# A graph layer's first attention step: the threshold guess formed as a logarithm, three guards in front of the mask, and list places found with one comparison

## The chip, the cores and the metric

The kernel runs on one NeuronCore of a Trainium2 chip. The time is that of the device in microseconds (us), from the start of the execution to its end; each time below is the median of several runs, or belongs to one profiled execution where that is said. The engines are TensorE (PE; PEld is its weight load), VectorE (DVE), ScalarE (ACT), GpSimd (POOL) and SyncE (SP, which here only issues DMAs).

## The reference

3327 nodes have 256 features each. The layer normalises the rows, cuts them at zero, and sends them through two steps of a graph layer; each step does this:

```
q = Xa @ W1.T @ W2.T;  k = Xa @ W3.T            # 64 wide
probs = softmax(q @ k.T)                         # 3327 x 3327
keep the largest entries of each row until their sum reaches 0.9; renormalise
Xf = R @ Xf        # R: the sparse adjacency plus identity, rows normalised
Xa = A @ Xa        # A: the kept probabilities
Z += Xf @ U1[n].T + Xa @ U2[n].T
```

At the end comes a layer norm of X + Z and a residual. So each row needs a threshold: the value from which on its entries are kept. The adjacency has only a few nonzero entries in each row; the kernel finds them as lists and fetches the few blocks it needs.

## The kernel before, in words

The nodes are cut into 26 tiles of 128 rows (the last one has fewer). Two steps follow each other: step 0 (about 60 to 745 us of the profiled execution) and step 1 (from there to the end). Only step 0 is touched here.

In step 0 each tile t goes through these stages, and the loop of `guess_graph_layer` over i keeps several tiles in flight at once:

- **weights** (L583 to L610): PE forms the logits `pl`, ACT takes their exponential into `e` (128 x 3328) and sums each row.
- **measured_once** (L635 to L666): ACT guesses from the row's sum Z and a fitted law where the threshold may lie (`guessed`, L616 to L625, and L640 to L642, one number per row in the columns of a small tile `g`); GpSimd prepares four more numbers (L643 to L646); ACT then makes two whole passes over `e` (L633: Relu and Sign, each with a row sum), which tell the mass below the guess. Seven small ACT operations (L653 to L659) turn this into a better guess, and five small VectorE operations (L662 to L666) add guards and write it to column 16.
- **settle** (L723 to L767): VectorE takes the part of `e` below the guess into `w` (L729), finds its largest entries by MAX8 over 20 segments (L734) and five rounds over the candidates (L741, L743), derives from them the exact threshold (L748 to L753), and cuts the row with it, the **mask** (L763, in place in `e`).
- **Sums** (L809 to L832): PE transposes the masked `e` four blocks at a time into `pt` (L809), ACT copies them to `eT` (L811), PE multiplies them with the nodes into `pa` (L823).
- **first_end** and **prep** (L474 to L502, L937 to L949): products with U2, new keys and queries (`pz`, `pk`, `pg`).

Beside this the adjacency is turned into lists. `listed` (L836 to L868) reduces the blocks of `adj` that SP loads, and leaves up to 16 neighbour numbers per row in `lists`; the first four are fetched directly, further ones by an overflow column that all rows share. VectorE counts a row's overflow entries into `over` (L865). `packed` (L870 to L880) turns the counts into places: PE adds the counts of the rows before (`pb`, with the matrix `upto`), and VectorE writes a 0/1 matrix `oh` with two comparisons, so that oh[row, n] is 1 where the row's first place <= n < first place + count. `gathered` (L882 to L894) multiplies with `oh` on PE (`po`), ACT copies the result (`lo` L888, `nth` L890), VectorE picks (L893), GpSimd writes the index (L894). GpSimd then issues indirect DMAs: five per tile for adjacency blocks (`ac`, L900) and five for node rows (`xg`, L921). `diffuse` multiplies the two (`pr`, L929), and `spread` finishes on VectorE (L1118, L1119).

The order of the work on each engine is the order of the text: at the end of `guess_graph_layer` every instruction of PE, ACT, VectorE and GpSimd is tied to the one before it. Each letter of the strings in PLAN and BEGIN stands for one stage and runs it up to its next `yield`; a tile of step 0 has seven such strings. The letters that count here are m (measured_once), d (settle), p (packed), h (gathered), g (one indirect DMA, which also waits for the ACT instruction that precedes it in the text), w and q (weights). A stage that has pieces left at the end of a turn is run out there. So the last piece of m, VectorE's guards, ran at the end of a turn, behind the mask of the tile before.

The pool `ps_t` has two PSUM buffers, which `pt`, `po`, `pq`, `pk`, `pg`, `pb` use in turn; so PE's `pk` (L485) waits until ACT has copied `mq` out of `pq` (L532), and a `pt` behind `po` waits for `nth`.

If any row's threshold can't be proved, a flag makes the program run a second, slow layer (`search_graph_layer`) at the end.

Of the kernel before, what the change touches and what calls it, by code (L numbers as in the profile page):

```python
# [9 lines left out]
F32 = mybir.dt.float32  # L10
# [3 lines left out]
AF = mybir.ActivationFunctionType  # L14
ALU = mybir.AluOpType
# [3 lines left out]
P = 128  # L19
# [4 lines left out]
NP = NT * P  # L24
# [288 lines left out]
BIG = 1.0e30  # L313
# [6 lines left out]
OFFSET = (18.0, 14.0)  # L320
TOPK = 8 * max(ROUNDS)
LNY = 0.25 * math.log(0.72)

SQG, SQK = ((c[0], c[1] / (2 * c[0]), c[2] - c[1] ** 2 / (4 * c[0])) for c in (PG, PK))
# [12 lines left out]
DIRECT = 4  # L337
LIST = 16
# [7 lines left out]
def guess_graph_layer(ctx, tc, x, adj, w1t, w2t, w3t, u1t, u2t, ln_g, ln_b, out, flag):  # L346
# [18 lines left out]
    valid = lambda t: 0 <= t < NT  # L365
# [47 lines left out]
    one = const.tile([P, 8], F32, tag="one", name="one")  # L413
    for k, c in enumerate((1.0, -1.0, 5.0e-4, SQG[1], SQK[1], math.log(10.0), LNY, 1.0e-12)):
        G.memset(one[:, k : k + 1], c)
# [212 lines left out]
    def con(k):  # L628
        return one[:, k : k + 1]
# [5 lines left out]
    def measured_once(r):  # L635
# [200 lines left out]
    def listed():  # L836
# [10 lines left out]
        for k, (t, j0, n) in enumerate(pieces):  # L847
# [6 lines left out]
            if j0 + n < NT:  # L854
# [9 lines left out]
            of = small.tile([P, LIST], F32, tag="of", name="of", bufs=2)  # L864
# [3 lines left out]
            yield  # L868

    def packed(t):  # L870

        assert t in done
# [3 lines left out]
        S.copy(ls[:, LIST:], pb[:, 0, :1])  # L876
        yield
        ohs[t] = oh = small.tile([P, P], F32, tag="oh", name="oh", bufs=2)
        V.tensor_scalar(oh, place, ov, ls[:, LIST:], ALU.subtract, ALU.is_lt)
        V.scalar_tensor_tensor(oh, place, ls[:, LIST:], oh, ALU.is_ge, ALU.mult)  # L880

    def gathered(t):  # L882
# [10 lines left out]
        V.scalar_tensor_tensor(of[:, :n], place[:, :n], nth, lo, ALU.is_equal, ALU.mult, accum_out=nth)  # L893
        G.tensor_scalar(index[:, t, DIRECT:], nth, -1.0, float(NONE), ALU.mult, ALU.add)  # L894
# [88 lines left out]
    live, ohs, acs, xgs, done, early = {}, {}, {}, {}, [], {}  # L983
# [45 lines left out]
    for q in range(HALF + 5):  # L1029
# [40 lines left out]
        if 0 <= q - 4 < HALF and 2 * (q - 4) in COUNTED:  # L1070
            k = q - 4
# [54 lines left out]
    def refetch(t):  # L1126
# [9 lines left out]
    PLAN = (("gmdsssa", "gmcdsssa", "edawwpg", "gmsdga", "gmspdea", "ohgdawwqg", "gehmgq"),  # L1136
# [5 lines left out]
             0: ("mdbb", "mcdbb", "medbwwbp", "mdbb", "gmpdbwwb", "hgdbgbq", "hgq"),  # L1142
             1: ("ggmdsssbb", "gmcdgsssbb", "gedbwwbp", "bmsdg", "gmpdeg", "hgdwwqg", "hgemgqo"),
             2: ("gmdsssa", "gmcdsssga", "gedawwpg", "gmsdga", "gmspdea", "ohgdawwqg", "gehmgq")}
# [136 lines left out]
```

## Time and profile before

| | us |
|---|---|
| median of 3 runs | 1347.66 (1346.17 to 1348.82) |
| the profiled execution, its own time | 1349.25 |
| its span, first to last instruction | 1347.5 |
| busy in the span: PE, PEld | 1269.8 (94%), 975.5 (72%) |
| busy in the span: DVE, ACT, POOL | 1187.0 (88%), 1080.0 (80%), 1002.8 (74%) |
| chain that ended last, by engine | PE 50%, DVE 27%, ACT 14%, POOL 3%, issue 3%, DMA 2% |

The granted TensorE clock was 0.982 of full speed as a mean. A row of the profile names line, engine and operation, then output<-input, how often, the busy time in us, the mean duration in ns, and the idle time of the engine ahead of it with what ended it. The chain of waits follows the last instruction back to what it waited for. Everything that concerns step 0 is read from the windows between 0 and 745 us.

### The profile page before, as it was taken

To read this page: it belongs to the slowest core of one execution; us is meant where nothing else is said; L and a number is where in the kernel's file an instruction comes from. 1 tells how busy PE (TensorE), PEld (TensorE's weight loads), DVE (VectorE), ACT (ScalarE), POOL (GpSimd) and SP (SyncE) were. 2 spreads that over 40 slices of the span, in tenths; PEclk is the share of its full clock that TensorE was granted. 3 is DMA by queue.
4 is the path that set the end of the run, shared out by engine and by line. 5 is a ranking of instruction groups with operands and counts; after the bars stand their busy time and mean duration, and the time that the engine had idled before them with its cause. 6 is when DMAs were issued, how large, how long until landed. Compare 5 with 4: busy or idle time off the path is not lost.

```text
span 1347.5 us, 22277 instructions
## 1 busy us (share of the span) xinstructions
PE 1269.8 (94%) x6495; PEld 975.5 (72%) x6495; DVE 1187.0 (88%) x3637; ACT 1080.0 (80%) x2368; POOL 1002.8 (74%) x1399
## 2 busy tenths in 40 slices
PE   5989999999999999999999579999998999999985
PEld 4635777778777787777877457777777777777774
DVE  6867899999999999999991699899998999999993
ACT  5476798888878888888853889899998999999931
POOL 5214888888888888887873588888888888888822
PEclk9999999999999999999999789999999999999988
DMA  8734455454554545545432212121222212122100
GB/s 278 226 124 140 133 146 158 133 159 128 140 158 132 156 135 144 151 135 149 122 105 82 81 48 83 55 90 55 92 77 65 87 56 91 59 86 89 54 20 24
DMA packets 92645, 149.79 MB, mean 111 GB/s; under 512 B 15425, under 2 KB 59072, under 8 KB 92512
## 3 DMA queue, kind: packets, MB, share of 16 engines
q1 hardware_dynamic: 75056, 105.37, 24.7%
q0 software_dynamic: 16640, 42.69, 12.4%
q8 instruction: 54, 0.88, 0.3%
q14 instruction: 79, 0.65, 0.2%
q10 hardware_dynamic: 816, 0.20, 0.1%
HBM read 120.93 MB, written 27.28 MB: 110 GB/s over the span
## 4 chain that ended last, share of the span: by engine, by line
PE 50%; DVE 27%; ACT 14%; POOL 3%; issue 3%; DMA 2%; SPq 0%; POOLq 0%; DVEq 0%; ACTq 0%
PE pa L823 22%; ACT ja L633 7%; PE pl L600 7%; PE pt L809 6%; DVE w L729 5%; PE pr L929 5%; DVE cand L734 4%; DVE e L763 4%; PE pz L942 3%; DVE bb L741 2%; DVE cand L743 2%; DVE x L763 2%; PE pz L1011 2%; ACT eT L811 1%; ACT e L604 1%
## 5 line engine op out<-in xcount | busy, mean ns | idle before, releaser
L823 PE MATMUL pa<-xw,eT 128*128 128x256 f32 x1352 | 323.1, 383 | 3.3 <-DVE s L953 3.3
L633 ACT ACTIVATE ja<-e,g 128x3328 uint8<-128x3328 f32 x106 | 325.8, 3073 | 0.1
L823 PE MATMUL pa<-x,eT 128*128 128x256 f32 x1352 | 322.0, 379 | 0.0
L823 PEld LDWEIGHTS pa<-xw,eT 128*128 128x128 f32 x1352 | 250.5, 190 | 52.0 <-issue 14.4
L823 PEld LDWEIGHTS pa<-x,eT 128*128 128x128 f32 x1352 | 242.8, 190 | 25.5
L734 DVE MAX8 cand<-w 128x8 f32<-128x168 f32 (+1 forms) x1040 | 253.3, 317 | 0.0
L921 POOL DMA_INDIRECT xg<-bx,index x130 | 200.9, 1546 | 52.8 <-issue 24.4
L811 ACT COPY eT<-pt 128x512 f32<-128x512 f32 (+1 forms) x364 | 199.8, 556 | 46.6 <-PE pt L809 45.9
L809 PE MATMUL pt<-ident,e 128*128 128x128 f32 x1144 | 177.0, 277 | 16.8 <-DVE e L760 9.3
L900 POOL DMA_INDIRECT ac<-in_adj,index x130 | 147.8, 1137 | 58.4 <-issue 26.6
L809 PEld LDWEIGHTS pt<-ident,e 128*128 128x128 f32 x1144 | 140.3, 145 | 60.3 <-issue 33.1
L729 DVE SCALAR_TENSOR_TENSOR w<-e,g 128x3328 f32<-128x3328 f32 x44 | 163.4, 3715 | 2.8 <-ACT g L714 2.7
L921 POOL DMA_INDIRECT xg<-vx,index x130 | 133.3, 1025 | 34.1 <-issue 30.0
L763 DVE SCALAR_TENSOR_TENSOR e<-e,rec 128x3328 f32<-128x3328 f32 x40 | 151.3, 3782 | 0.6
L929 PE MATMUL pr<-xg,ac 128*128 128x257 f32 (+1 forms) x520 | 142.4, 398 | 8.2 <-DVE s L1119 6.5
L604 ACT ACTIVATE e<-pl 128x832 f32<-128x832 f32 x132 | 112.9, 859 | 22.4 <-PE pl L600 19.0
L929 PEld LDWEIGHTS pr<-xg,ac 128*128 128x128 f32 x520 | 94.7, 196 | 34.3 <-issue 14.4
L600 PE MATMUL pl<-both,qT 64*128 64x416 f32 x416 | 93.0, 546 | 8.0 <-ACT e L604 4.3
L741 DVE MAX8 bb<-cand 128x8 f32<-128x160 f32 x286 | 92.6, 324 | 6.4
L600 PE MATMUL pl<-after,qT 64*128 64x416 f32 x416 | 95.7, 554 | 0.5 <-ACT e L604 0.5
L853 DVE TENSOR_REDUCE fm<-at 128x4 f32<-128x512 f32 (+1 forms) x133 | 84.3, 634 | 0.3 <-DMA at<-in_adj 0.3
L946 POOL TENSOR_TENSOR sv<-sv,x 128x256 f32<-128x256 f32 x26 | 65.5, 2518 | 13.4 <-ACT sv L945 12.1
(260 smaller groups left out, 2163.4 us busy)
## 6 DMA issues: line engine op xcount, KB each, us to landing
at<-in_adj SPq DMA_DIRECT2D x114, 256.0 KB
cx<-ac SPq DMA_DIRECT2D x26, 384.0 KB
ac<-cx SPq DMA_DIRECT2D x26, 384.0 KB
wide<-in_adj SPq DMA_DIRECT2D x8, 832.0 KB
e<-in_adj SPq DMA_DIRECT2D x6, 832.0 KB
own<-bx SPq DMA_DIRECT2D x26, 128.5 KB
x<-in_x SPq DMA_DIRECT2D x13, 256.0 KB
xr<-in_x SPq DMA_DIRECT2D x26, 128.0 KB
```

The lines of the kernel that those rows point to most:

```text
L600: PE.matmul(pl[:, a, :wd], qT[p, :], keys_of(step, a).rearrange("p a b -> p (a b)")[:, c : c + wd], start=True, stop=True)
L604: S.activation(e.rearrange("p (a n) -> p a n", a=2)[:, :, c : c + wd], pl[:, :, :wd], AF.Exp, accum_out=za[:, n : n + 1])
L633: S.activation(ja, e, f, bias=guess, scale=sign, accum_out=total)
L729: V.scalar_tensor_tensor(w, e, col(16), e, ALU.is_lt, ALU.mult, accum_out=d2)
L734: V.max(cand[:, 8 * s : 8 * s + 8], w[:, s * SEG : min(NP, (s + 1) * SEG)])
L763: V.scalar_tensor_tensor(e, e, at(1), e, ALU.is_ge, ALU.mult, accum_out=ra)
L809: PE.transpose(pt[:, j, :], e[:, (j0 + j) * P : (j0 + j + 1) * P], ident)
L811: S.copy(eT[:, :w, :], pt[:, :w, :])
L823: PE.matmul(self.pa, eT[:, c - 4 * k, :], self.xa[:, j, :], start=c == 0, stop=c == NT - 1)
L900: G.indirect_dma_start(out=ac[:, k, :], out_offset=None, in_=rows, in_offset=bass.IndirectOffsetOnAxis(ap=index[:, t, k : k + 1], axis=0), ...
L921: G.indirect_dma_start(out=xg[:, k, :w], out_offset=None, in_=rows, in_offset=bass.IndirectOffsetOnAxis(ap=index[:, t, k : k + 1], axis=0))
L929: PE.matmul(pr[:, :w], ac[:, k, :], own if k == KT - 1 else xg[:, k, :w], start=k == 0, stop=k == KT - 1)
```

## The change

Part 1, the guess. Its last steps are made with logarithms and one exponential. ScalarE's Square term is left out, the offset is 19 where it was 18, and the guards become amounts that are subtracted from an exponent where they were huge numbers that were added. GpSimd prepares eight numbers where it prepared four; some of them share columns with what ScalarE writes behind its second pass. VectorE has three guard operations where it had five, and ScalarE's last two operations (Relu, Exp) now come behind them.

Part 2, the place in the order. An m is added to the sixth string of each turn, behind h and in front of d: VectorE's guards and ScalarE's last two operations are in the text in front of the mask.

Part 3, the lists. The count moves from VectorE to ScalarE (Sign with a row sum) and, for most tiles, to a later place (the end of `gathered` two tiles earlier). GpSimd forms half the count and its square, ScalarE adds an offset from `pb` and squares the distance of each place from the middle, and VectorE compares once.

```diff
-OFFSET = (18.0, 14.0)
+OFFSET = (19.0, 14.0)
...
         S.activation(col(1), col(0), AF.Exp, scale=-1.0, bias=con(5))
+        G.tensor_scalar(col(11), col(11), -1.0, None, ALU.mult)
         G.tensor_scalar(col(7), col(9), 0.5, None, ALU.mult)
...
+        G.tensor_scalar(col(12), col(3), ms(3), ms(8), ALU.mult, ALU.add)
+        G.tensor_scalar(col(12), col(12), -1.0, 80.0, ALU.mult, ALU.add)
+        G.tensor_scalar(col(13), r["Z"], 0.035, None, ALU.mult)
         yield
...
         S.activation(col(6), col(4), AF.Ln, scale=col(1), bias=con(2))
-        S.activation(col(3), col(4), AF.Square, scale=col(1), bias=con(1))
-        S.activation(col(3), col(3), AF.Ln, scale=0.5, bias=col(10))
-        S.activation(col(3), col(3), AF.Identity, scale=-1.0, bias=col(6))
-        S.activation(col(3), col(3), AF.Exp, scale=col(11))
-        yield
-
-        V.tensor_scalar(col(5), oa[:, 1:2], NP - 31.0, BIG, ALU.is_gt, ALU.mult)
-        V.tensor_scalar(col(6), col(4), col(1), 0.35, ALU.mult, ALU.is_lt)
-        V.scalar_tensor_tensor(col(5), col(6), BIG, col(5), ALU.mult, ALU.add)
-        V.tensor_scalar(col(3), col(3), 1.0e20, col(9), ALU.min, ALU.mult)
-        V.tensor_tensor(col(16), col(3), col(5), ALU.add)
+        S.activation(col(10), col(10), AF.Ln)
+        S.activation(col(10), col(10), AF.Identity, scale=-1.0, bias=col(6))
+        yield
+        V.tensor_scalar(col(5), oa[:, 1:2], NP - 31.0, 60.0, ALU.is_gt, ALU.mult)
+        V.tensor_scalar(col(14), col(4), col(13), 60.0, ALU.is_lt, ALU.mult)
+        V.scalar_tensor_tensor(col(12), col(12), col(5), col(14), ALU.subtract, ALU.subtract)
+        S.activation(col(10), col(10), AF.Relu, scale=col(11), bias=col(12))
+        S.activation(col(16), col(10), AF.Exp, scale=-1.0, bias=con(8))
...
-            V.tensor_scalar(of[:, DIRECT:], ls[:, DIRECT:LIST], 0.0, None, ALU.is_gt, ALU.add,
-                            accum_out=over[:, t : t + 1])
...
+    def counted(t):
...
+        S.activation(of[:, DIRECT:], lists[:, t, DIRECT:LIST], AF.Sign, accum_out=ov)
+        nhs[t] = nh = small.tile([P, 3], F32, tag="nh", name="nh", bufs=4)
+        G.tensor_scalar(nh[:, 0:1], ov, -0.5, 0.5, ALU.mult, ALU.add)
+        G.tensor_scalar(nh[:, 1:2], ov, ov, 0.25, ALU.mult, ALU.mult)
...
         S.copy(ls[:, LIST:], pb[:, 0, :1])
-        yield
+        S.activation(nh[:, 2:3], pb[:, 0, :1], AF.Identity, scale=-1.0, bias=nh[:, 0:1])
         ohs[t] = oh = small.tile([P, P], F32, tag="oh", name="oh", bufs=2)
-        V.tensor_scalar(oh, place, ov, ls[:, LIST:], ALU.subtract, ALU.is_lt)
-        V.scalar_tensor_tensor(oh, place, ls[:, LIST:], oh, ALU.is_ge, ALU.mult)
+        S.activation(oh, place, AF.Square, bias=nh[:, 2:3])
+        yield
+        V.tensor_scalar(oh, oh, nh[:, 1:2], None, ALU.is_lt)
...
+        if valid(t + 2):
+            counted(t + 2)
         G.tensor_scalar(index[:, t, DIRECT:], nth, -1.0, float(NONE), ALU.mult, ALU.add)
...
-    PLAN = ((..., "ohgdawwqg", "gehmgq"), ...)
+    PLAN = ((..., "ohgmdawwqg", "gehmgq"), ...)
-             0: (..., "hgdbgbq", "hgq"), 1: (..., "hgdwwqg", "hgemgqo"), 2: (..., "ohgdawwqg", ...)
+             0: (..., "hgmdbgbq", "hgq"), 1: (..., "hgmdwwqg", "hgemgqo"), 2: (..., "ohgmdawwqg", ...)
```

In the built programs PE's and SP's instructions and their order are the same as before; ACT has 78 instructions more, VectorE 104 fewer and GpSimd 157 more (six more per tile, and one at the start).

More of the change, by code (lines that the diff above doesn't have):

```diff
@@ L412, in guess_graph_layer @@
     law = const.tile([P, 7, NT], F32, tag="law", name="law")
-    one = const.tile([P, 8], F32, tag="one", name="one")
-    for k, c in enumerate((1.0, -1.0, 5.0e-4, SQG[1], SQK[1], math.log(10.0), LNY, 1.0e-12)):
+    one = const.tile([P, 9], F32, tag="one", name="one")
+    for k, c in enumerate((1.0, -1.0, 5.0e-4, SQG[1], SQK[1], math.log(10.0), LNY, 1.0e-12, 80.0)):
         G.memset(one[:, k : k + 1], c)
@@ L863, in listed @@
             G.tensor_scalar(index[:, t, :DIRECT], ls[:, :DIRECT], -1.0, float(NONE), ALU.mult, ALU.add)
-            of = small.tile([P, LIST], F32, tag="of", name="of", bufs=2)
-            V.tensor_scalar(of[:, DIRECT:], ls[:, DIRECT:LIST], 0.0, None, ALU.is_gt, ALU.add,
-                            accum_out=over[:, t : t + 1])
             done.append(t)
             yield
+    def counted(t):
+        if t not in done or t in nhs:
+            return
+        of = small.tile([P, LIST], F32, tag="of", name="of", bufs=2)
+        ov = over[:, t : t + 1]
+        S.activation(of[:, DIRECT:], lists[:, t, DIRECT:LIST], AF.Sign, accum_out=ov)
+        nhs[t] = nh = small.tile([P, 3], F32, tag="nh", name="nh", bufs=4)
+        G.tensor_scalar(nh[:, 0:1], ov, -0.5, 0.5, ALU.mult, ALU.add)
+        G.tensor_scalar(nh[:, 1:2], ov, ov, 0.25, ALU.mult, ALU.mult)
     def packed(t):
-        assert t in done
+        counted(t)
+        nh = nhs[t]
         ls, ov = lists[:, t, :], over[:, t : t + 1]
@@ L876, in packed @@
         S.copy(ls[:, LIST:], pb[:, 0, :1])
+        S.activation(nh[:, 2:3], pb[:, 0, :1], AF.Identity, scale=-1.0, bias=nh[:, 0:1])
+        ohs[t] = oh = small.tile([P, P], F32, tag="oh", name="oh", bufs=2)
+        S.activation(oh, place, AF.Square, bias=nh[:, 2:3])
         yield
-        ohs[t] = oh = small.tile([P, P], F32, tag="oh", name="oh", bufs=2)
-        V.tensor_scalar(oh, place, ov, ls[:, LIST:], ALU.subtract, ALU.is_lt)
-        V.scalar_tensor_tensor(oh, place, ls[:, LIST:], oh, ALU.is_ge, ALU.mult)
+        V.tensor_scalar(oh, oh, nh[:, 1:2], None, ALU.is_lt)
     def gathered(t):
@@ L982, in guess_graph_layer @@
     own_of = {}
-    live, ohs, acs, xgs, done, early = {}, {}, {}, {}, [], {}
+    live, ohs, acs, xgs, done, nhs, early = {}, {}, {}, {}, [], {}, {}
     none = iter(())
@@ L1129, in refetch @@
         yield from fetched(vx, t, D)
-    PLAN = (("gmdsssa", "gmcdsssa", "edawwpg", "gmsdga", "gmspdea", "ohgdawwqg", "gehmgq"),
+    PLAN = (("gmdsssa", "gmcdsssa", "edawwpg", "gmsdga", "gmspdea", "ohgmdawwqg", "gehmgq"),
             ("llcmss", "lnms", "lwwnfd", "lcmdsssgggg", "fdsmwqdf", "llmdf", "lmwdg"))
@@ L1141, in guess_graph_layer @@
     BEGIN = {-1: ("mba", "mmbba", "mwwbbaa", "bmwwb", "", "", ""),
-             0: ("mdbb", "mcdbb", "medbwwbp", "mdbb", "gmpdbwwb", "hgdbgbq", "hgq"),
-             1: ("ggmdsssbb", "gmcdgsssbb", "gedbwwbp", "bmsdg", "gmpdeg", "hgdwwqg", "hgemgqo"),
-             2: ("gmdsssa", "gmcdsssga", "gedawwpg", "gmsdga", "gmspdea", "ohgdawwqg", "gehmgq")}
+             0: ("mdbb", "mcdbb", "medbwwbp", "mdbb", "gmpdbwwb", "hgmdbgbq", "hgq"),
+             1: ("ggmdsssbb", "gmcdgsssbb", "gedbwwbp", "bmsdg", "gmpdeg", "hgmdwwqg", "hgemgqo"),
+             2: ("gmdsssa", "gmcdsssga", "gedawwpg", "gmsdga", "gmspdea", "ohgmdawwqg", "gehmgq")}
     OPEN = {-1: ("llcmss", "lnms", "lwwnfd", "lcmdsssggggg", "fmgdswqdf", "llmdf", "lmwfdm"),
```

## The prediction

> **What bounds the kernel now.** I first read the windows, to see which engine fills which stretch of step 0, since only step 0 changes.
>
> ```profile
> 60.00:100.00 40.00, 33.41 (x92) 13.42 (x90) 27.93 (x90) 30.19 (x63) 9.85 (x27) 0.96 0.43 140
> 100.00:147.00 47.00, 44.13 (x184) 28.16 (x185) 36.75 (x102) 30.77 (x73) 25.58 (x34) 1.00 0.46 135
> 147.00:347.00 200.00, 200.00 (x1067) 158.08 (x1066) 191.33 (x597) 170.20 (x419) 167.46 (x198) 1.00 0.51 144
> 347.00:547.00 200.00, 199.10 (x1064) 157.12 (x1063) 193.14 (x595) 166.37 (x418) 170.85 (x192) 1.00 0.51 146
> 547.00:700.00 153.00, 152.72 (x811) 120.30 (x810) 147.38 (x458) 124.56 (x304) 127.45 (x144) 1.00 0.46 131
> ```
>
> After the stretch and its length come busy us of PE, PEld, DVE, ACT, POOL. From 147 to 700 us PE is idle for 0.00 + 0.90 + 0.28 = 1.2 us. A modelled busy PE could still hide waits, so I looked at the chain of waits there: it is PE alone, and its pieces run at an even rate (eight records of `pa` in 1.73 us each time). A tile takes 23.35 or 24.20 us by turns (the odd turns have `pg` and L488), from which few tiles stray. VectorE is busy for 96% too, but PE does not wait for it. So in the middle of step 0 nothing that is taken off VectorE can bring more than about 1.2 us. The start (60 to 147 us) is different: PE idles for 6.6 + 2.9 us, and the chain goes through VectorE, ScalarE, GpSimd and DMAs. I read its end in the timelines of DVE, ACT, POOL and PE, put together here:
>
> ```profile
> 128.68 3.69 DVE L763 SCALAR_TENSOR_TENSOR e<-e,rec 128x3328 f32<-128x3328 f32 x1
> 131.55 0.39 ACT L654 ACTIVATE g<-oa,g 128x1 f32<-128x1 f32 x1
> 132.86 0.94 POOL L921 DMA_INDIRECT xg<-bx,index  x1 [10.01 <-DMA own<-bx]
> ...
> 136.61 0.95 POOL L921 DMA_INDIRECT xg<-bx,index  x1 [0.30 <-ACT mq L532]
> 136.80 3.67 DVE L729 SCALAR_TENSOR_TENSOR w<-e,g 128x3328 f32<-128x3328 f32 x1
> 137.86 3.43 POOL L921 DMA_INDIRECT xg<-bx,index  x1 [0.30 <-issue]
> ...
> 143.94 0.70 PE L929 MATMUL pr<-xg,ac 128*128 128x257 f32 x2 [1.72 <-DMA xg<-bx,index]
> ```
>
> The five `xg` issues of the first tile run at 1.25 us each while VectorE has no whole-row operation; the one that begins inside L729 takes 3.43 us. PE then waits 1.72 us for its landing. From there on PE never stops, so what is lost at 144 us is lost at the end.
>
> Last, ScalarE around PE's `pk`, in two tiles:
>
> ```profile
> 205.86 0.27 ACT L890 ACTIVATE nth<-po,part 128x1 f32<-128x1 f32 x1
> 208.24 0.30 ACT L532 COPY mq<-pq 128x130 f32<-128x130 f32 x1
> 209.29 0.61 PE L485 MATMUL pk<-xT,wk 128*128 128x128 f32 x4
> ...
> 349.97 0.27 ACT L890 ACTIVATE nth<-po,part 128x1 f32<-128x1 f32 x1
> 352.08 0.32 ACT L532 COPY mq<-pq 128x130 f32<-128x130 f32 x1
> 352.45 0.71 PE L485 MATMUL pk<-xT,wk 128*128 128x128 f32 x4
> ```
>
> `pk` needs the buffer that `mq` frees. In the first tile the copy ends 0.75 us ahead of it, in the second 0.05 us.
>
> **The change part by part.** VectorE, per tile: the guards were 145 + 200 + 184 + 205 + 160 = 894 ns, three of these forms are about 145 + 205 + 184 = 534; L880 (351) and the count (166 + 83) go. Together 0.96 us less. In the middle this is off the path; the bound is the 1.2 us of PE idle time, of which I take 1.0.
>
> ScalarE, per tile: four operations (373 + 294 + 295 + 295) become four (Ln 295, Identity 387, Relu 387 as L641, Exp 295); added are Sign with its row sum (as L620, 209 + 191), an Identity out of PSUM (267, as L890) and a Square over 128 columns. For the Square no row is the same: an SBUF to SBUF pass of that width lies between a single column (294) and the copy of 256 columns (375). The Trainium skill (ScalarE: Activation LUTs, What ACT_TABLE_LOAD costs) puts a pass with a pointer bias at about 280 ns plus 0.833 ns per column: an estimate of 387, just above the rows' bracket. I take 0.35; by the rule it is 0.04 more, nothing that decides. In all 1.1 us more, where ScalarE idles for 3.5 us a tile (29.8 of 200 us, 23.8 us a tile), most of it waiting for PE. Whatever the place, the idle time covers it, except where PE waits soon behind: Sign (in front of L811 or L620), Identity and Square (behind L876) have a second PSUM buffer and 2 us or more before PE comes back to theirs. Relu and Exp do not: they stand between L890 and L604, and `mq` is four operations behind. Small ACT operations follow each other at 0.33 us when dependent and 0.20 when not, so 0.53 us come in front of `mq`. I read the gap from `mq` to `pk` in the timelines of 20 tiles, from 180 us on: 0.75 in six, 0.3 to 0.7 in six, 0.2 or less in eight. The shortfalls against 0.53 add up to 4.4 us. But the gaps are short where `lo` (L888) starts late, and that is mostly where VectorE has fallen behind PE by a few tenths; with 0.96 us less work it won't. Bounds 0 and 4.4 us; I take 1.5, nearer the early tiles, whose VectorE is where it will be.
>
> GpSimd, per tile: four numbers (about 0.9 us with L643, L646 as the rows) and two for the counts (0.4): 1.3 us more. It idles for 3.9 us a tile, of which about 0.3 stand in front of each of ten indirect DMAs and are not free. Yet a GpSimd operation that meets L763 or L729 stands for up to 4.2 us (L946 at 348.83 did, until 353.00), and arriving later it stands for less. `xg` of a tile is issued 11 us ahead of `pr`. So nothing on the path in the middle. ScalarE's L653 now also waits for GpSimd's sixth number (it overwrites a column that this reads); the slack from L646 to L653 was 2 to 3.5 us, and only at 656.8 us none: 0.3 us there.
>
> Moved: the guards stand in front of the mask. What is queued behind the waiting guard on VectorE is the mask, and for the mask PE waits. In the middle ScalarE's L654 ends about 3 us before the mask, so it costs nothing. At the start it does not. In the excerpt above the mask runs at 128.68, while the sums of the next tile are known only at 131.94 (end of L654). PE wants that mask only at 136.85, so PE is not held; GpSimd is. I first sum the delays ahead: the comparison for tile 0 waits for ScalarE's Square (from 63.92 to about 64.4, and through SP and the load of `wide` that VectorE waits for until 73.22: +0.35, less 0.2 for the count); L729 at 78.33 now waits for Relu and Exp (+0.75, less 0.3 for shorter guards); this goes through L1017 to PE at 89.73: +0.6. Sign in front of L620 at 109.19: +0.25. Identity and Square in front of L811 at 126.23: +0.3. Sum 1.15 us.
>
> So L654 ends at 133.1, the guards at 133.7, the mask runs to 137.5. The first `xg` (132.86 + 1.15 to 1.25) comes at 134.1 and stands inside it until about 138.3; the second goes at 138.6, when L729 starts too; one of second and third stands until 143.1; the rest follow at 1.25 us. The last ends at 145.6 to 146.9, where the delay alone gives 142.4. If the first slips past the mask, only one more stands: 143.7. Bounds 1.3 and 4.4 us; I take 3.0. Here a rule speaks against me: the Trainium skill (SBUF — State Buffer, Who interferes with whom) holds that a VectorE operation with two SBUF inputs shuts out only GpSimd's reads, and infers that writing descriptors is not among these. By it the indirect DMAs would not stand and this term would be 0. The row (3.43 us in L729 against 0.95 in the others) decides.
>
> Sum: start 1.15 + 3.0, middle -1.0 + 1.5, end +0.3: +5.0 us. The profiled span of 1347.5 becomes 1352.5; its run took 1349.25 with 1.75 outside the span, 1.6 above the median, so I put the difference on the median: 1352.7.
>
> **Rivals.** *The start lets it pass.* The indirect DMAs slip between mask and L729, or the skill's inference holds: start +1.15, ScalarE's insertion is covered since VectorE is early (0), PE's idle time goes (-1.2): 1347.6, not slower. For it: 136.61 began 0.19 us before L729 and was not held. It decides at whether `xg` is issued before the mask starts. Against it: by my sum it comes 0.4 us too late. *ScalarE uncovered.* `lo` stays as late as now for a reason that is not VectorE: 4.15 + 4.4 + 0.3 = +8.9: 1356.5. For it: the delay of `lo` is not explained by any row. *GpSimd becomes the bound.* Between mask and L729 lay 1.7 us, now 1 us, so an `xg` that ran there (353.16) stands; 1.25 + 1.3 us more against at most 3.4 us of standing that can shrink. If 1 us a tile is missing: 24 tiles and the start's 4.15, 1376. *It does not do what it says*: if one row's guess misses, the slow layer runs and the time multiplies. The formula differs only by a small offset and a term that is small near the target; below 1%.
>
> **How the numbers follow.** Forecast 0.47 (1350.5 to 1355), start passes 0.33, ScalarE uncovered 0.13, GpSimd 0.07. The range of 8 in 10 goes from 1346.6 (the second case with only 0.2 us at the start) to 1357.5. Within 0.2% (2.7 us, about what a measurement can tell from no change) is 1345.0 to 1350.4: most of the second case, 0.27; faster 0.07; slower 0.66.
>
> **What would show it.** Right: the mask near 128.68 moved to 133 or later, one or two `xg` of the first tile over 3 us, PE's wait near 144 us 4 us or so longer; PE's idle time from 150 us on still about 1 us per 200; tiles at 23.35 and 24.20. Wrong: `xg` issues of 0.95 us throughout; gaps in front of `pk` in most tiles (ScalarE's case); PE waiting for `xg` in every tile (GpSimd's); or a shorter start, which would mean that VectorE's saved time was on the path there.

## The result, and the profile after

The changed kernel takes 1388.34 us (median, 1387.08 to 1389.2), the kernel before 1348.21 beside it: a ratio of 1.03 [1.0282, 1.0317]. It is 40 us slower, where 5 us were forecast and the range ended at 1357.5. The profiled execution of the changed kernel took 1389.07 us, with a span of 1387.3 at a mean granted clock of 0.979 (before 0.982). Line numbers from L657 on have moved: the mask is now L764, the whole-row operation behind it L730, `ac` L913, `xg` L934, `pr` L942, `sv` L959, the copy `eT` L812.

The windows of the changed kernel, over the stretches shown of before (PE, PEld, DVE, ACT, POOL busy, then clock, DMA share, GB/s):

```profile
60.00:100.00 40.00, 32.72 (x84) 13.45 (x84) 24.83 (x69) 28.80 (x64) 9.35 (x36) 0.91 0.39 125
100.00:147.00 47.00, 41.59 (x162) 23.92 (x160) 34.62 (x93) 29.04 (x79) 27.47 (x31) 0.98 0.41 128
147.00:347.00 200.00, 197.22 (x1030) 154.36 (x1031) 175.34 (x526) 167.94 (x435) 171.33 (x233) 0.99 0.47 135
347.00:547.00 200.00, 191.83 (x1001) 146.63 (x1000) 174.92 (x530) 163.88 (x424) 171.30 (x235) 1.00 0.47 139
547.00:700.00 153.00, 145.49 (x752) 109.88 (x751) 131.12 (x398) 123.17 (x315) 128.69 (x177) 1.00 0.47 135
```

PE, which idled for 1.2 us between 147 and 700 us, now idles for 2.78 + 8.17 + 7.51 = 18.5 us there and gets less done at the same time (1030 matmul records in a stretch that held 1067). VectorE fell from 191 to 175 busy us per 200: its work shrank, and fewer tiles fall into a stretch. Only GpSimd is fuller: 171.3 in both long stretches, where it had 167.5 and 170.9.

I measured where the 40 us arise from the starts of the 24 whole-row masks of step 0 (tiles 0 and 25 have theirs in two pieces), in the two profiled executions. The 5th comes 8.9 us later than before (237.5 against 228.6), the 23rd 35.5 later (695.9 against 660.4), the 24th and last 40.7 later (723.6 against 682.9). So 9 us arise at the start, 26.6 us over the 18 tiles of the middle (25.47 us a tile in place of 23.99, mean of 18), and 5 us between the last two masks. Step 1 adds nothing.

The waits of the changed kernel between 150 and 700 us (who waited <- for whom: us in total, times, longest):

```profile
DVE fm L854 <- DMA at<-in_adj: 47.8, 19, 4.2
ACT g L657 <- POOL g L648: 37.1, 18, 2.9
PEld pk L485 <- ACT mq L532: 17.8, 17, 1.9
PE pk L485 <- ACT mq L532: 10.9, 17, 1.5
```

None of these rows existed before in such a size. (PEld's wait for `mq` and PE's are the same 17 waits, seen on both rows.) All of them lead to GpSimd: ScalarE's first operation behind its second pass (L657) waits for GpSimd's sixth number (L648); `mq` is late because ScalarE is; and the adjacency blocks `at` are loaded by SP behind a store of `sv`, which GpSimd sums (L959). The chain, which was PE for 50% of the span, now reads:

```profile
DVE 37%; PE 22%; ACT 19%; POOL 12%; issue 6%; DMA 3%; SPq 0%; POOLq 0%; DVEq 0%; ACTq 0%
```

One tile of the changed kernel, from the timelines of POOL, DVE and ACT (start, duration, engine):

```profile
360.69 0.29 ACT L657 ACTIVATE g<-oa,g 128x1 f32<-128x1 f32 x1 [2.52 <-POOL g L648]
363.12 0.95 POOL L913 DMA_INDIRECT ac<-in_adj,index  x1 [0.30 <-ACT sv L958]
363.24 3.67 DVE L764 SCALAR_TENSOR_TENSOR e<-e,rec 128x3328 f32<-128x3328 f32 x1
364.38 3.35 POOL L913 DMA_INDIRECT ac<-in_adj,index  x1 [0.31 <-issue]
367.91 3.68 DVE L730 SCALAR_TENSOR_TENSOR w<-e,g 128x3328 f32<-128x3328 f32 x1
368.04 4.38 POOL L913 DMA_INDIRECT ac<-in_adj,index  x1 [0.30 <-issue]
...
373.69 0.74 POOL L959 TENSOR_TENSOR sv<-sv,x 128x256 f32<-128x256 f32 x1
377.72 0.42 DVE L854 TENSOR_REDUCE fm<-at 128x2 f32<-128x256 f32 x1 [2.59 <-DMA at<-in_adj]
```

Two `ac` issues stand back to back, one in the mask and one in L730. Behind them `sv` is late, behind `sv` the loads, and VectorE waits 2.59 us for them. Before, it was mostly `sv` and one `xg` that stood, one issue passed in the gap between the two whole-row operations, and GpSimd was earlier by a few us. A tile of the kernel before, from the same timelines:

```profile
372.56 3.68 DVE L763 SCALAR_TENSOR_TENSOR e<-e,rec 128x3328 f32<-128x3328 f32 x1
373.38 3.44 POOL L946 TENSOR_TENSOR sv<-sv,x 128x256 f32<-128x256 f32 x1
376.97 0.97 POOL L921 DMA_INDIRECT xg<-bx,index  x1
377.94 3.68 DVE L729 SCALAR_TENSOR_TENSOR w<-e,g 128x3328 f32<-128x3328 f32 x1
378.24 4.21 POOL L921 DMA_INDIRECT xg<-bx,index  x1 [0.30 <-ACT both L494]
```

In the rows of the groups from 150 to 700 us the mean of an `ac` issue is 2126 ns (before 1154) and that of an `xg` 1037 (before 1584); first the two rows of before, then those of the changed kernel:

```profile
L900 POOL DMA_INDIRECT ac<-in_adj,index x116 | 133.9, 1154 | 32.7 <-issue 24.0 <-ACT g L654 1.5 <-ACT ja L633 1.2
L921 POOL DMA_INDIRECT xg<-bx,index x118 | 186.9, 1584 | 37.9 <-issue 22.9 <-ACT eT L811 3.4 <-ACT g L654 3.3
L913 POOL DMA_INDIRECT ac<-in_adj,index x107 | 227.5, 2126 | 29.3 <-issue 14.9 <-ACT sv L958 5.0 <-ACT g L641 1.5
L934 POOL DMA_INDIRECT xg<-bx,index x110 | 114.0, 1037 | 31.5 <-issue 17.6 <-ACT g L658 4.1 <-ACT g L666 2.8
```

The start went as the prediction described, somewhat worse. From the same timelines and PE's:

```profile
135.27 3.68 DVE L764 SCALAR_TENSOR_TENSOR e<-e,rec 128x3328 f32<-128x3328 f32 x1
135.56 4.21 POOL L934 DMA_INDIRECT xg<-bx,index  x1 [6.74 <-DMA own<-bx]
139.36 3.68 DVE L730 SCALAR_TENSOR_TENSOR w<-e,g 128x3328 f32<-128x3328 f32 x1
140.08 3.78 POOL L934 DMA_INDIRECT xg<-bx,index  x1 [0.30 <-issue]
...
146.67 0.95 POOL L934 DMA_INDIRECT xg<-bx,index  x1 [0.30 <-issue]
145.72 1.23 PE L942 MATMUL pr<-xg,ac 128*128 128x257 f32 x2 [3.04 <-DMA xg<-bx,index]
147.41 1.23 PE L942 MATMUL pr<-xg,ac 128*128 128x257 f32 x2 [0.47 <-DMA xg<-bx,index]
```

Here the granted clock plays a part too. It is at about half for 3 us from 74 us on in both kernels (0.50 before, 0.53 changed), and in the changed kernel twice more; the same stretches of the changed kernel and then of before:

```profile
81.00:84.00 3.00, 3.00 (x5) 1.20 (x4) 0.97 (x3) 2.90 (x7) 1.24 (x6) 0.56 0.00 0
146.00:149.00 3.00, 2.53 (x7) 1.51 (x8) 3.00 (x13) 0.00 (x0) 2.32 (x6) 0.50 0.58 139
```

```profile
81.00:84.00 3.00, 3.00 (x9) 1.33 (x8) 2.70 (x7) 3.00 (x3) 1.77 (x4) 1.00 0.01 3
146.00:149.00 3.00, 3.00 (x17) 1.75 (x15) 2.90 (x13) 1.10 (x3) 2.44 (x7) 1.00 0.53 127
```

The 5 us between the last two masks are mostly one wait, from the timelines of ACT, POOL and PE:

```profile
710.98 0.21 ACT L874 ACTIVATE of<-lists 128x12 f32<-128x12 f32 x1
717.62 0.21 POOL L876 TENSOR_SCALAR nh<-over 128x1 f32<-128x1 f32 x1
717.87 0.26 ACT L887 ACTIVATE nh<-pb,nh 128x1 f32<-128x1 f32 x1 [5.96 <-POOL nh L876]
718.18 0.83 PE L810 MATMUL pt<-ident,e 128*128 128x128 f32 x4 [4.24 <-ACT nh L887]
```

For this tile the count (L874) is made only in `packed` itself. GpSimd forms half of it (L876) 6.6 us later, behind what is in front of it in the text; ScalarE's Identity (L887) waits for that, and PE's transposes wait for ScalarE.

### The profile page after: what moved, and what is told of

Same layout as the page of the kernel before. It is cut to its first block, busy times and chain, and to the rows that moved or that the text cites. A ratio compares the mean times of both kernels' runs of the same rounds, so it can differ in the third digit from the quotient of the medians.

```text
span 1387.3 us, 22431 instructions
## 1 busy us (share of the span) xinstructions
PE 1284.2 (93%) x6495; PEld 974.5 (70%) x6495; DVE 1162.2 (84%) x3507; ACT 1096.7 (79%) x2472; POOL 1045.1 (75%) x1556
## 4 chain that ended last, share of the span: by engine, by line
DVE 37%; PE 22%; ACT 19%; POOL 12%; issue 6%; DMA 3%; SPq 0%; POOLq 0%; DVEq 0%; ACTq 0%
PE pa L824 8%; ACT ja L633 8%; DVE w L730 6%; DVE cand L735 6%; DVE e L764 5%; POOL ac L913 4%; DVE bb L742 3%; POOL xg L934 3%; DVE cand L744 3%; PE pt L810 2%; PE pl L600 2%; PE pz L1024 2%; DMA at<-in_adj 2%; PE pr L942 2%; ACT e L604 2%
## 5 line engine op out<-in xcount | busy, mean ns | idle before, releaser
L913 POOL DMA_INDIRECT ac<-in_adj,index x130 | 255.6, 1966 | 50.8 <-issue 17.9
L824 PEld LDWEIGHTS pa<-xw,eT 128*128 128x128 f32 x1352 | 250.2, 190 | 51.9 <-issue 14.4
L812 ACT COPY eT<-pt 128x512 f32<-128x512 f32 (+1 forms) x364 | 198.2, 552 | 48.9 <-PE pt L810 48.3
L934 POOL DMA_INDIRECT xg<-bx,index x130 | 142.8, 1098 | 44.6 <-issue 20.7
L730 DVE SCALAR_TENSOR_TENSOR w<-e,g 128x3328 f32<-128x3328 f32 x44 | 162.4, 3692 | 3.5 <-ACT g L715 2.7
L934 POOL DMA_INDIRECT xg<-vx,index x130 | 133.7, 1028 | 34.0 <-issue 29.8
L942 PE MATMUL pr<-xg,ac 128*128 128x257 f32 (+1 forms) x520 | 143.7, 401 | 11.5 <-DVE s L1132 7.6
L764 DVE SCALAR_TENSOR_TENSOR e<-e,rec 128x3328 f32<-128x3328 f32 x40 | 147.5, 3688 | 0.6
L942 PEld LDWEIGHTS pr<-xg,ac 128*128 128x128 f32 x520 | 95.3, 197 | 39.0 <-issue 15.4
L678 POOL TENSOR_SCALAR g<-g 128x1 f32<-128x1 f32 x26 | 73.4, 2823 | 1.8
```

The source lines that it names most:

```text
L730: V.scalar_tensor_tensor(w, e, col(16), e, ALU.is_lt, ALU.mult, accum_out=d2)
L764: V.scalar_tensor_tensor(e, e, at(1), e, ALU.is_ge, ALU.mult, accum_out=ra)
L812: S.copy(eT[:, :w, :], pt[:, :w, :])
L824: PE.matmul(self.pa, eT[:, c - 4 * k, :], self.xa[:, j, :], start=c == 0, stop=c == NT - 1)
L913: G.indirect_dma_start(out=ac[:, k, :], out_offset=None, in_=rows, in_offset=bass.IndirectOffsetOnAxis(ap=index[:, t, k : k + 1], axis=0), ...
L934: G.indirect_dma_start(out=xg[:, k, :w], out_offset=None, in_=rows, in_offset=bass.IndirectOffsetOnAxis(ap=index[:, t, k : k + 1], axis=0))
```

## The experiments

Each version is built on one of the two kernels ("before", "changed"). Ratios are to runs of the kernel before on the same chip (medians of 1349.4 to 1351.8 us); "span" and the tile figures are those of the profiled execution.

**First round: parts alone.** I had three theories: GpSimd's work and missing room (G), ScalarE's late Relu and Exp (A), the guards' place ahead of the mask (P).

*a_nomove*: the changed kernel with the old strings (no m between h and d). Expected:

> The changed kernel with the order strings of the kernel before: the guards, Relu and Exp run behind the mask again. Theory G (GpSimd bounds step 0: six more small operations a tile, 1.3 us, and only 1.0 us of room between mask and L730) expects that the room comes back to about 1.5 us but the six operations stay: about 1365, between 1355 and 1380. Theory P (the place in front of the mask is the whole loss) expects 1349 or less. Theory A (ScalarE's Relu and Exp in front of the exponentials delay mq and so PE's pk) expects 1349 too, since they leave that place.

Measured 1383.52 us, 1.024 [1.0223, 1.0257]. *b_move*: the kernel before with the m added, nothing else. Expected:

> The kernel before with the guards in front of the mask alone (five VectorE operations; no GpSimd and no ScalarE operation more). Theory G expects some loss from the lost room, since an indirect DMA less gets through between mask and L729: 1350 to 1365. Theory P expects about 1388. Theory A expects 1348, since ScalarE has nothing in that place.

Measured 1359.69, 1.0076 [1.0046, 1.0106]. So the place is worth some 10 us when it is alone, within G's range; a_nomove lies above all three expectations, since taking the place back in the changed kernel wins only 5 us (8 by the ratios). L730 then waits for ScalarE's Relu (L666), which follows guards that follow the mask: 10.6 us in 15 tiles.

*a_nogp*: the changed kernel without its six GpSimd operations. VectorE forms the four numbers of the guess beside its guards, ScalarE those of the counts, and ScalarE no longer overwrites column 3.

```diff
-        G.tensor_scalar(col(11), col(11), -1.0, None, ALU.mult)
...
+        V.tensor_scalar(col(11), col(11), -1.0, None, ALU.mult)
...
-        G.tensor_scalar(nh[:, 0:1], ov, -0.5, 0.5, ALU.mult, ALU.add)
-        G.tensor_scalar(nh[:, 1:2], ov, ov, 0.25, ALU.mult, ALU.mult)
+        S.activation(nh[:, 0:1], ov, AF.Identity, scale=-0.5, bias=half[:, 1:2])
+        S.activation(nh[:, 1:2], ov, AF.Square, scale=0.5)
-        S.activation(col(3), oa[:, 0:1], AF.Identity, scale=-1.0, bias=col(8))
+        S.activation(col(15), oa[:, 0:1], AF.Identity, scale=-1.0, bias=col(8))
```

> The changed kernel without its six added GpSimd operations per tile: the four numbers of the guess are formed on VectorE beside the guards, the two of the counts on ScalarE, and ScalarE's first operation behind its second pass writes a column that GpSimd does not read. Theory G expects most of the 40 us back: 1350 to 1362. Theories P and A expect no gain, 1388 or more, since place and ScalarE's work stay (ScalarE has two more operations).

Measured 1355.68, 1.0035 [1.0022, 1.0049]. Its windows in the middle:

```profile
147.00:347.00 200.00, 198.44 (x1043) 157.05 (x1044) 184.20 (x580) 172.28 (x451) 162.83 (x197) 0.98 0.50 144
347.00:547.00 200.00, 199.46 (x1061) 157.09 (x1060) 192.18 (x603) 177.59 (x465) 167.54 (x200) 1.00 0.50 144
```

PE is full again, and a tile takes 23.97 us, though VectorE and ScalarE have more to do than in the changed kernel. So 33 of the 40 us (36 by the ratios) hang on the six GpSimd operations and the waits for them.

*b_load*: the kernel before with six idle GpSimd operations per tile at those places (short ones, 4 x 191 + 2 x 204 ns = 1.17 us by their rows). Expected:

> The kernel before with six idle GpSimd operations per tile at the places of the six that the change adds; their results are not used. Theory G expects that GpSimd, with the room between mask and L729 as before, gets slower by part of 1.3 us a tile: 1355 to 1380. If GpSimd's time inside VectorE's whole-row operations can shrink, as the prediction held, 1348. Theories P and A expect 1348.

Measured 1349.18, 0.9987 [0.9972, 1.0002]: no loss at all. That seemed to refute G and left the waits (theory W): the six operations cost because somebody waits for them.

**Second round: the waits.** *a_free* gives ScalarE a column of its own, so that L657 no longer waits for L648:

```diff
-        S.activation(col(3), oa[:, 0:1], AF.Identity, scale=-1.0, bias=col(8))
-        S.activation(col(4), oa[:, 1:2], AF.Relu, scale=col(7), bias=col(3))
+        S.activation(col(15), oa[:, 0:1], AF.Identity, scale=-1.0, bias=col(8))
+        S.activation(col(4), oa[:, 1:2], AF.Relu, scale=col(7), bias=col(15))
```

> The changed kernel with one thing undone: ScalarE's first operation behind its second pass (L657) writes a column of its own and no longer the column that GpSimd's sixth number reads, so it no longer waits for GpSimd; all six added GpSimd operations stay. Theory W (it is this wait that costs, because it hands GpSimd's delay on to ScalarE): the wait of L657 for L648 is gone, and the loss shrinks from 38 us to what the version without the six GpSimd operations showed, 1352 to 1358. Theory G (the load and the missing room of GpSimd cost): no change, 1380 to 1390. Theory L (the loads of the adjacency that come late hold VectorE by themselves): between, 1365 to 1380, with VectorE's wait for the loads at 20 us or more.

Measured 1385.23, 1.0249 [1.0227, 1.0272]. Theory W fell at once; the time is in G's range. The waits of this version say why:

```profile
DVE fm L854 <- DMA at<-in_adj: 44.2, 18, 4.1
ACT g L666 <- DVE g L665: 22.4, 19, 2.1
PEld pk L485 <- ACT mq L532: 20.4, 17, 2.0
ACT g L657 <- POOL g L645: 18.4, 16, 1.8
```

L657 now waits for the number that it always needed (L645, as before L644). GpSimd is late by as much as it was; the tie was only where this showed. *a_free_nomove* is the same with the old strings:

> As the version without that wait, and with the old place of the guards (behind the mask). W: what is left is the price of the place at most, so it goes to 1346 to 1350, as the kernel before. If the place costs nothing once the wait is gone: the same as the version with the new place, within 2 us. G: as the changed kernel with the old place, about 1383.

Measured 1384.88, 1.0237 [1.0218, 1.0256]; W's 1346 to 1350 is out, and the time is that of a_free within 2 us and near what G said. *b_load_tied* is b_load with one idle operation reading the column that ScalarE overwrites:

> The kernel before with six idle GpSimd operations per tile (which alone cost nothing: 1349.18), where one of them, the sixth in GpSimd's group, now reads the column that ScalarE overwrites behind its second pass, so that ScalarE waits for it as in the changed kernel. W: this one tie brings the loss, 1370 to 1385, with ScalarE's wait for that GpSimd operation among the largest. G: as without the tie, 1347 to 1351. If the tie needs the new place of the guards to do harm: 1349 to 1360.

Measured 1348.21, 0.9971 [0.9957, 0.9985], against a median of 1351.75 of that session, whose runs of the kernel before lay between 1347.0 and 1355.8; I read it as no loss. A tie without lateness costs nothing. *b_lists* has the change of the lists alone on the kernel before:

> The kernel before with the change of the lists alone (count on ScalarE, half the count and its square on GpSimd, Square on ScalarE, one comparison on VectorE). W: GpSimd's two numbers are needed only in the next string, so little waits for them: 1345 to 1352. G: as W. If the second tie, ScalarE's Identity behind the product with the counts that waits for GpSimd's half count, is one that hands the delay on: 1360 or more, with ScalarE waiting for L876's successor.

Measured 1358.3, 1.005 [1.0036, 1.0065], between the two expectations. Most of its loss is late in step 0 (PE 185.78 us from 547 to 740, before 191.86). The tie of the half count shows in one of the last tiles, as in the changed kernel: ScalarE's Identity waits 4.4 us for it, and PE 2.7 us behind it.

**Third round: the amount.** Two theories were left: R, that the amount of GpSimd's work exceeds its room, and T, that the waits cost. By their rows in the changed kernel the six operations take 264 + 355 + 195 + 210 ns (guess) and 207 + 270 (counts): 1.50 us, a third of a microsecond more than my idle ones. *b_same6* puts these very forms into the kernel before, results unused:

> The kernel before with the very six GpSimd operations that the change adds, at the same places and of the same forms (1.50 us per tile by the rows of the changed kernel, where the six idle ones were 1.17), results unused. Theory R (GpSimd's room: it can take some 1.2 us per tile because what stands inside VectorE's whole-row operations shrinks, and no more): the excess of 0.3 us or more per tile shows, 1357 to 1385. Theory T (load costs nothing in itself; in the changed kernel it is the waits for these numbers that carry GpSimd's delay to ScalarE and VectorE): 1347 to 1351.

Measured 1374.41, 1.0178 [1.0154, 1.0201], in R's range. *a_nogp_same6* puts them into a_nogp, results unused:

> The version of the changed kernel in which VectorE and ScalarE form the six numbers (1355.68), with the six GpSimd operations put back, results unused. R: the load is that of the changed kernel and the gap between the mask and the next whole-row operation is short as there, so the loss comes back, 1375 to 1390. T: nothing waits for them, so 1354 to 1358.

Measured 1385.22, 1.0272 [1.0233, 1.031]: nearly the whole loss is back, and nothing needs these results. A tile takes 25.48 us, as in the changed kernel (25.47), so in the middle the waits for them don't matter. The 5 us between the last two masks are not there: they hang on the half count, which ScalarE forms in this version. The windows of b_load and of b_same6 between 147 and 547 us, first b_load:

```profile
147.00:347.00 200.00, 198.73 (x1058) 156.54 (x1057) 191.41 (x594) 168.74 (x412) 171.44 (x249) 1.00 0.49 143
347.00:547.00 200.00, 199.15 (x1066) 157.40 (x1065) 193.08 (x596) 167.59 (x421) 172.10 (x240) 1.00 0.50 146
```

and b_same6:

```profile
147.00:347.00 200.00, 197.22 (x1044) 155.21 (x1043) 185.41 (x565) 164.73 (x405) 171.10 (x229) 0.99 0.48 136
347.00:547.00 200.00, 191.64 (x1000) 150.03 (x999) 184.38 (x566) 159.04 (x395) 171.46 (x234) 0.99 0.47 137
```

GpSimd's busy time is the same 171 in both; the rest of the 200 is mostly the short idle time in front of its DMAs. It is full in both, but in the second PE falls back, 8.4 us in the second stretch. A busy share therefore can't tell a GpSimd that just fits from one that doesn't. *a_guess_v* and *a_counts_s* take one of the two groups off GpSimd in the changed kernel:

> The changed kernel with the four numbers of the guess formed by VectorE; half the count and its square stay on GpSimd (0.48 us per tile). R: well under the room, so as with none of the six on GpSimd, 1354 to 1359. T: the two ties of the counts stay (GpSimd waits for ScalarE's Sign, ScalarE's Identity waits for GpSimd's half count): between, 1358 to 1372, as the change of the lists alone cost 0.5%.

> The changed kernel with the two numbers of the counts formed by ScalarE; the four of the guess stay on GpSimd (1.03 us per tile). R: inside the room of 1.2 us that the six idle operations showed, so 1354 to 1360, unless the shorter gap behind the mask has taken some of it. T: the four ties of the guess stay, so most of the loss stays, 1370 to 1385.

Measured 1367.5, 1.0128 [1.0104, 1.0152] with 0.48 us left, and 1370.41, 1.0157 [1.0129, 1.0185] with 1.02 us left. Both of R's numbers were missed (it allowed a free 1.2 us). Both times lie in T's ranges, the second at the edge, but T had fallen with b_same6 and a_nogp_same6, and about half of the loss stays, not most of it. The loss grows with the amount: there is next to no room left in the changed kernel.

**Fourth round: what else hangs on it.** *b_load8* is b_load with eight idle operations (1.55 us):

> The kernel before with eight idle GpSimd operations per tile, all of the short form that in the number of six cost nothing (1.17 us per tile); eight are 1.55 us by the same rows, as much as the six in kind (1.50 us, 1374.4). Theory R1 (the amount decides: the room ends between 1.17 and 1.50 us): 1365 to 1385. Theory R2 (the forms or the place of the six decide, such as the operation ahead of the group): 1347 to 1352.

Measured 1363.0, 1.0096 [1.0072, 1.012]. The amount does count, but it lies under R1's range: at nearly the same time the six in kind cost 11 us more. *a_sx* moves SP's store of `sv` behind the diagonal block's load:

```diff
-        nc.sync.dma_start(sx[t], sv)
+        pend.append(lambda: nc.sync.dma_start(sx[t], sv))
...
                 nc.sync.dma_start(ac[:, KT - 1, :], adj[t, :, t, :])
+                while pend:
+                    pend.pop(0)()
```

> The changed kernel with one DMA of each tile, SP's store of sv (which waits for GpSimd's sum and is in front of loads of the adjacency), put behind the diagonal block's load, so that those loads no longer wait for GpSimd. If this loop (late GpSimd, late store, late loads, late VectorE) makes the loss greater than GpSimd's excess: 1360 to 1375, with VectorE's wait for the loads under 15 us. If GpSimd's own time sets the period: 1383 to 1390, whatever the loads do.

Measured 1381.97, 1.024 [1.0215, 1.0265]. VectorE's wait for the loads is no longer among the largest, yet only 6 us came back (8 by the ratios), and the time lies 1 us below the second expectation; ScalarE's wait for L648 is 41.3 us. So the late loads, the largest row of the waits, were a consequence. *a_sv* gives the sum `sv` to VectorE, straight from PSUM:

> The changed kernel, its six GpSimd operations and all waits for them kept, with another GpSimd operation of each tile taken away: the sum sv (0.9 us when it doesn't stand) is made by VectorE straight from PSUM, and ScalarE's copy in front of it goes too. R: GpSimd's load is 0.6 us above that of before, so most of the loss goes, 1354 to 1368. If the new operations hurt by who waits for them and not by their time: 1380 or more.

Measured 1381.99, 1.0239 [1.0213, 1.0265]. This is outside R's range and inside the other; but the run decides nothing about the load, since the new operation brought a wait of its own, and the `ac` issues stood for still longer:

```profile
DVE sv L958 <- ACT xw L956: 37.1, 21, 3.1
```

```profile
L913 POOL DMA_INDIRECT ac<-in_adj,index x109 | 240.5, 2207 | 30.0 <-issue 14.6 <-ACT xw L956 3.3 <-ACT of L874 2.7
```

*a_nogp_nomove* is a_nogp with the old strings:

> The changed kernel with GpSimd's six numbers formed by VectorE and ScalarE (1355.7) and the guards at the old place, behind the mask. If what remained there is the place (PE idle in the start because the moved mask makes the first indirect DMAs stand): 1348 to 1352. If it is the rest of the change (ScalarE's longer chain, Square in front of the comparison): 1354 to 1358.

Measured 1367.31, 1.0132 [1.0105, 1.016], worse than either expectation: with Relu and Exp behind the guards, and these behind the mask, L730 waits for L667 22 times, 17.3 us. The new place and the new order of ScalarE's chain belong together.

**Fifth round.** *a_nosv* leaves the sum `sv` out and gives it to nobody:

```diff
-        G.tensor_tensor(sv, sv, x0[:, t, :], ALU.add)
```

> The changed kernel with all its six GpSimd operations and waits, and GpSimd's sum sv of each tile (0.93 us when it doesn't stand) left out: sv holds ScalarE's copy alone, so that the stored rows lack x. No other engine gets anything to do for it. Room theory: GpSimd's load is 0.57 us above that of before, near the version with the counts' numbers alone (0.48 us, 1367.5): 1358 to 1372. If the new operations hurt by their waits or their place: 1380 or more.

Measured 1365.52, 1.0107 [1.0082, 1.0133], with the six operations and all waits for them still there. The middle is repaired:

```profile
147.00:347.00 200.00, 200.00 (x1066) 158.76 (x1065) 181.25 (x551) 174.46 (x447) 168.99 (x236) 1.00 0.51 144
347.00:547.00 200.00, 199.06 (x1060) 157.08 (x1058) 186.24 (x557) 174.26 (x449) 169.39 (x239) 1.00 0.51 147
```

PE is as full as before the change. What it lacks is at the start (73.82 us of PE from 60 to 147, before 77.54) and behind 547 us, mostly the wait for the half count (PE idle for 4.0 us). *b_move_load* combines b_move and b_load on the kernel before:

> The kernel before with both the new place of the guards (alone 1359.7, 10 us more) and the six idle GpSimd operations (alone 1349.2, nothing more). Room theory: the place shortens the gap between the mask and the next whole-row operation from 1.9 to 1.1 us and so takes the room in which the six were free; 1.17 us per tile for 24 tiles come on top, 1375 to 1390. If the two don't touch each other: 1357 to 1362.

Measured 1370.12, 1.0144 [1.0116, 1.0172]. Alone the place costs about 10 us and the six idle operations nothing; together they cost 20. So the place does take part of GpSimd's room, but not all of it (1375 to 1390 was expected).

The table puts the versions side by side. The tile is the mean of the 18 from the 5th to the 23rd mask, and GpSimd's time per tile in them is split into what stands, idle time, and its own work. What stands is what an indirect issue takes beyond 0.96 us, `sv` beyond 0.93 and the index operations beyond 0.2. The start is the shift of the 5th mask. All but the ratio are from one execution each.

| kernel | GpSimd added, us | own work, us | stands, us | idle, us | tile, us | 5th mask later by | ratio |
|---|---|---|---|---|---|---|---|
| before | 0 | 13.9 | 6.4 | 3.7 | 23.99 | 0 | 1 |
| b_load | 1.17 | 15.0 | 5.8 | 3.2 | 23.99 | 2.0 | 0.9987 |
| b_load8 | 1.55 | 15.6 | 6.2 | 3.1 | 24.86 | 2.2 | 1.0096 |
| b_same6 | 1.50 | 15.5 | 6.1 | 3.6 | 25.18 | 4.2 | 1.0178 |
| b_move | 0 | 13.9 | 6.2 | 4.2 | 24.20 | 6.5 | 1.0076 |
| b_move_load | 1.17 | 15.0 | 6.5 | 3.1 | 24.64 | 7.9 | 1.0144 |
| b_lists | 0.48 | 14.4 | 6.3 | 3.6 | 24.33 | 0.4 | 1.005 |
| a_nogp | 0 | 13.9 | 6.2 | 3.9 | 23.97 | 9.9 | 1.0035 |
| a_nogp_nomove | 0 | 13.9 | 5.9 | 4.7 | 24.44 | 10.5 | 1.0132 |
| a_nosv | 0.57 | 14.6 | 5.9 | 3.7 | 24.18 | 4.5 | 1.0107 |
| a_guess_v | 0.48 | 14.3 | 6.5 | 3.7 | 24.50 | 8.6 | 1.0128 |
| a_counts_s | 1.02 | 14.9 | 6.2 | 3.5 | 24.69 | 7.8 | 1.0157 |
| a_nogp_same6 | 1.50 | 15.5 | 6.4 | 3.6 | 25.48 | 7.9 | 1.0272 |
| a_nomove | 1.50 | 15.3 | 6.3 | 3.6 | 25.24 | 6.4 | 1.024 |
| changed | 1.50 | 15.5 | 6.4 | 3.6 | 25.47 | 8.9 | 1.03 |

In every version of the table two GpSimd operations per tile stand (36 in the 18 tiles; 35 in b_move), and they stand for 5.8 to 6.5 us together, however much GpSimd has to do.

No version beats the kernel before: its middle is bound by PE with 1.2 us of idle time, as the prediction had it, and none of the parts shortens the start.

## Why the prediction was wrong, point by point

**The step that failed** is GpSimd's: "1.3 us more", of which what stands inside VectorE's operations "can shrink" ("arriving later it stands for less"), "so nothing on the path in the middle". The amount was nearly right (1.50 by the rows). What was wrong is that it would be absorbed. What stands is 6.4 us a tile in both kernels: nothing shrank, it moved from `sv` (2.2 to 0 us) and `xg` (3.3 to 0.3) to `ac` (0.7 to 6.2). Whenever a whole-row operation starts while issues are queued, the next issue stands for it, however late GpSimd is. The idle time, mostly fixed gaps ahead of the DMAs, stayed at 3.6 of 3.7 us. So the 1.5 us of own work came out as 1.48 us of tile.

How much room there was: b_load took in its 1.1 us half by idle time (3.7 to 3.2) and half by standing (6.4 to 5.8), where the prediction counted on up to 3.4 us of standing that can shrink. With 0.4 to 0.5 us more (b_load8) the standing is back at 6.2, and the tile is 0.87 us longer. b_move_load has the own work and the idle time of b_load, and 0.7 us more standing: its tile is 0.65 us longer, the price of the shorter gap on a full GpSimd. On top of a_nogp the first 0.48 us already cost 0.5 (a_guess_v), 1.02 cost 0.7, and 1.50 cost 1.5. But the place alone is not it: with the old place the changed kernel still has a tile of 25.24 us.

**The rival "GpSimd becomes the bound"** named this mechanism, with 1 us a tile over 24 tiles and a total of 1376; I gave it 7 in 100. Measured are 1.48 us a tile. The row that should have raised its chance was on the page: GpSimd idled for 3.9 us a tile of which ten times 0.3 were known not to be free, so that less than 1 us was really free beside 1.3 new ones. The rest was hope in the elasticity of what stands. Its counter-argument, the lead of `xg` over `pr`, was true and beside the point: PE has no wait for `xg` from 150 to 700 us, in either kernel. GpSimd's lateness reached PE by other roads, the numbers L644 to L648 that ScalarE needs and the loads behind `sv`.

**"0.3 us there" for ScalarE's wait on GpSimd's sixth number.** The wait measured 37.1 us in 18 tiles. But it was no cause: without the tie the loss stayed (a_free), and the tie without the lateness cost nothing (b_load_tied). A tie that did cost was put at nothing: ScalarE's Identity on GpSimd's half count, 4.2 us of PE in one of the last tiles. That loss between the last two masks (5.2 us in the changed kernel, 5.8 in a_nosv, 2.9 in a_guess_v) is missing where ScalarE forms the half count (a_nogp, a_counts_s, a_nogp_same6).

**The start.** Forecast +4.15, of which 3.0 for `xg` that stand in the moved mask. The mechanism was right in its details: the first issue stands in the mask (4.21 us), a second in L730 (3.78), the last ends at 147.62, where 145.6 to 146.9 was worked out. The mask itself came at 135.27 instead of 133.7. PE's waits for `xg` there sum to 4.0 us (0.48 + 3.04 + 0.47), 2.3 more than before, where the prediction named about 4 as the sign. The size was too small: b_move alone has its 5th mask 6.5 us later, the changed kernel 8.9, a_nogp 9.9, and a_nogp loses nothing after it. A term that the prediction doesn't have is the granted clock: at about half for two further stretches of 3 us it costs some 1.5 us each, an estimate from the clock and from PE's being on the path there (busy for 3.00 and 2.53 us of the two stretches). That is about 3 of the missing 4.7 us; the rest, and what lets the clock fall, was not taken apart.

**VectorE and the middle.** That nothing taken off VectorE can bring more than 1.2 us there is not contradicted: in a_nosv VectorE is busy for 181 and 186 us per 200 (before 191 and 193), and PE's busy time is that of before. No run takes work off VectorE alone. The 1.0 us that was to be gained did not show: in a_nogp PE idles for 2.5 us from 150 to 700, before 1.2.

**ScalarE.** +1.5 us, with bounds 0 and 4.4. In a_nogp, where GpSimd's lateness is gone, PE idled for `mq` ahead of `pk` for 1.1 us in 2 tiles, before in none: inside the bounds, in a version that gives ScalarE two operations more still. The Square over 128 columns took 0.40 us (L889), nearer to the 0.387 worked out by the rule than to the 0.35 taken. In the changed kernel PE idles ahead of `pk` for 10.9 us in 17 tiles. I had named gaps in front of `pk` as the sign of ScalarE's case; here they were the sign of a ScalarE that GpSimd had made late.

**The rule on two-input operations.** The Trainium skill (SBUF — State Buffer, Who interferes with whom) was read as if it made the standing of an issue 0: it lets a two-input VectorE operation shut out GpSimd's reads, and infers that descriptor writing needs the write interface. The rows contradict this reading: two operations a tile stand. They need not contradict the page. An indirect issue also takes its index from SBUF, and what is held lies near its beginning: issues begun 0.07 to 0.9 us ahead of a whole-row operation ended in 0.94 to 1.03 us, though they ran on inside it. That it is the index is not shown. The row was rightly preferred, but applied only to the start and not to the middle.

**What stays open.** Why the six in kind cost 11 us more than eight idle ones of the same time. In the profiled executions, 13 us apart, 5.9 us of it lie in the 18 tiles, where it is GpSimd's idle time (3.6 against 3.1) and neither own work nor standing; 2.0 lie at the start, and 5.2 behind the last mask, which is mostly step 1, where the two don't differ. One of the six stands ahead of the numbers that ScalarE waits for, the idle ones all behind; that was not tried alone. Why b_lists loses 0.3 us a tile with 0.48 us added is open too, since it also adds work to ScalarE.

## What to carry to other kernels

An engine whose time consists of issues that stand in another engine's operations has no free time just because that standing is waste: count its reserve as the idle time that isn't a fixed gap, and compare it with what is added. Splitting its time per tile into own work, standing and idle time shows whether it is full. A full engine doesn't show in a busy share (171 of 200 with and without loss) nor as a wait of the bounding engine; look whether all new waits lead back to it, and then test it by taking other work off it, since undoing single waits (a_free, a_sx) only moves the place at which its lateness shows. A load test must have the size of the real load: six idle operations that were 0.33 us too short gave the opposite answer.

## What the runs showed of the hardware

An indirect DMA issue that GpSimd starts while VectorE runs a whole-row operation with two inputs in SBUF (3.68 us) ends 0.82 us after that operation, from wherever between 0.12 and 2.0 us into it the issue began. From 147 to 745 us there are 33 issues begun inside such an operation before and 46 in the changed kernel; the quartiles of this distance are 0.82 and 0.83 us in both. The exceptions are two in each kernel, all begun within the first 0.10 us of the operation: they took 0.95 to 0.97 us, as an issue alone does. So one that stands makes almost no progress while the operation runs. A gap of 1.0 us between two such operations, from which 0.82 go to the one that stood and 0.30 lie in front of the next, let none pass in the tile shown, where 1.7 us let one pass.
